# Moved heads third of four pairs in the last image, and layer 3's sums behind the next unit's values

## The chip, the core and the metric

The kernel runs on one core of a Trainium2 chip. A core has a matrix engine (TensorE, PE in the profile; PEld is its weight load), a vector engine (VectorE, DVE), an engine for functions such as exp (ScalarE, ACT), a slower general engine (GpSimd, POOL), and a queue processor that only issues DMAs (SyncE, SP). They share an on-chip memory of 128 partitions (SBUF); matmul results go to a small second memory of eight banks (PSUM). The metric is the device time of one execution in microseconds; a lower number is better.

## The reference, cut to what matters

The input x has 8 images of 384 channels of 32 x 32 points (1024 positions). Four layers are added to it in turn, each after a group normalisation. Two of them hold the change.

Layer 0 is a full attention in each image with 8 heads of 48 channels:

```
q, k, v = dwproj(gn(x))                       # depthwise 3x3, batch norm, gelu, 1x1
attn = softmax(q^T k * 48**-0.5)              # 1024 x 1024 for each head
out  = w_out @ (v attn^T);  x = x + bn(out)   # bn: statistics over all 8 images
```

Layer 3 is a deformable attention with 6 heads of 64 channels, whose keys and values come from 256 sampled points:

```
q = q_w @ gn(x);  offsets = conv5x5 stride 2 of q, norm, gelu, 1x1
k, v = kv_w @ bilinear_sample(gn(x), offsets)
x = x + proj_w @ (softmax(q^T k * 64**-0.5) v) + proj_b
```

Layer 1 (between them) mixes four small experts, layer 2 is a 3x3 depthwise and a 1x1 convolution.

## The kernel before

**Order of work.** The code is written in program order; a list scheduler then orders the instructions of each engine by what is ready in its own model, with earlier code preferred, and adds the waits.[...] ACT is kept as written in layer 0's attention.

**Layer 0's attention.** The loop over `steps` goes image by image (b), pair of heads (pr, 0 to 3), half of the 1024 query positions (h), and two blocks of 128 keys at a time (kc). Per step, `scores` of the next step gives four matmuls per block in row and column quarters (s, L638), ACT takes the exp (p, L645), and `weigh` multiplies by the values into two PSUM banks (pav, L653). A column of ones beside each head's values (number `HQ0` = 24 of each group of 32) gives the softmax sum. At the end of a half, `normalise` (L605) adds the two banks (L610, L611), transposes in blocks of 32 x 32 (L614), takes the reciprocal of the sum's column (L615), multiplies (L616) and transposes back (L621 or L624). The step's `todo` list holds other PE work (projections of the next pair, of the next image, `out_project` of the image before); up to four of them are taken at kc = 2.

**Moved heads.** A head has 48 channels, and two heads of a pair take 2 x 48 of 128 rows. Pair 3 therefore holds no rows of its own in `atts`: its q and k rows are gathered from the spare rows of pairs 0, 1 and 2 by `gather_last` (tile ql, two DMAs on SP after each projection), and its result `al` is put by `place_last` into rows 24 to 31 of each group of 32 in the three blocks of `atts`, with 12 small DMAs. `atts[b]` has three blocks of 128 rows, one for each of pairs 0 to 2. For the last half of the last image the 12 DMAs alternate between SP's and ACT's queue.

**Output projection.** `out_project(b, m, h)` loads xh (a piece of x, two buffers), multiplies `wo0` by `atts` (po, L590), copies po to ot (DVE, or ACT for the last image, L601), takes its statistics (bn_stats, L602), stores ot, and `cross` sums a product of xh and ot (L488, L489). For the last image, h = 0 is taken inside the last half's loop, h = 1 after the loop. Then a check of the reciprocals (okt, L742 to L748) decides, through a branch, whether a slow general form is run; it is not run here. `norms` then makes the batch norm of the whole output, the branch is passed, and layer 1 loads its weights (w1).

**Layers 1 to 3.** From here on the work of two images is interleaved by hand. `layer1(b+1)` is a list of 48 units of three matmuls each (ph, L1274; y, L1295). `layers(b)` is a generator of layers 2 and 3 that yields estimates of idle PE time. For images 0 to 5, each time the yields add up to `UNIT` = 2.6, one unit of layer 1 is put in. Image 6 is treated so only up to a marked point (`yield None`); its rest runs beside image 7's layers, two steps of 7 for one of 6, and image 7's rest runs alone.

**Layer 3's attention** has six units (pr, h) for each image. In unit u, GpSimd adds the two exps (p01, L1620), PE multiplies them by the values (pav, L1605, bank `vbank`, of which there is one), DVE transposes pav (tu, L1623), and PE makes the next unit's scores (s, L1589, two 64-row matmuls that can run side by side). After a yield, two matmuls by ones sum p01 (pss, L1631, in the same `vbank`), and DVE divides: transpose (L1636), reciprocal (L1638), product (L1639), transpose (L1642). p, p01 and other tiles come from one set of five buffers (`flat`), which the next image's o tiles use too. At last comes the output product (pf, L1694). In layer 2, DVE runs a 3x3 filter tap by tap (L1370), in layer 3 a 5x5 filter (off, L1485).

## Time and profile before

| | us |
|---|---|
| median of 3 runs | 3717.47 (3716.41 to 3720.61) |
| the profiled execution | 3716.66 |
| its span | 3714.9 |
| layer 0's attention ends (last pav) | 1799.67 |
| last matmul of layer 0's output | ends by 1817.1 |
| layer 1's first matmul | 1839.81 |
| one image of layers 1 to 3 (2061.84 to 2283.68) | 221.84 |
| image 7 alone, from its first scores | 3653.60 to the end |

Times in the profile count from the span's start. The kernel's whole time also has 1.76 us outside the span. A line of the profile names a code line, an engine, the operation, the tile written and the tiles read, the shape, and a count. A float32 matmul appears as two records, so six records are three matmuls. A shape such as 128*64 is the part of the array that a matmul uses; smaller parts can run side by side. The bracket gives idle time before an instruction and what ended it. Because matmul ends are modelled, a PE that is shown as busy can still be working below its rate.

### The profile page before, as it was taken

To read this page: it belongs to the slowest core of one execution; us is meant where nothing else is said; L and a number is where in the kernel's file an instruction comes from. 1 tells how busy PE (TensorE), PEld (TensorE's weight loads), DVE (VectorE), ACT (ScalarE), POOL (GpSimd) and SP (SyncE) were. 2 spreads that over 40 slices of the span, in tenths; PEclk is the share of its full clock that TensorE was granted. 3 is DMA by queue.
4 is the path that set the end of the run, shared out by engine and by line. 5 is a ranking of instruction groups with operands and counts; after the bars stand their busy time and mean duration, and the time that the engine had idled before them with its cause. 6 is when DMAs were issued, how large, how long until landed. Compare 5 with 4: busy or idle time off the path is not lost.

```text
span 3714.9 us, 39037 instructions
## 1 busy us (share of the span) xinstructions
PE 3598.4 (97%) x15587; PEld 1504.2 (40%) x15587; DVE 1810.6 (49%) x2827; ACT 1273.6 (34%) x1524; POOL 195.9 (5%) x162
## 2 busy tenths in 40 slices
PE   7999999999999999999799999999999999999888
PEld 3444333333333333333244444444344444444433
DVE  6776223232323232323336557564764657557564
ACT  2222354545444453544222321323222232322222
POOL 0000100000000000000000010100101010010111
PEclk9999999999999999999899999999999999999898
DMA  6776311121212021212350010110101001010000
GB/s 205 240 249 231 127 55 36 63 56 43 63 40 78 25 75 28 72 28 72 125 201 23 33 51 20 46 42 33 37 23 56 26 33 43 27 51 20 0 34 18
DMA packets 88178, 253.32 MB, mean 68 GB/s; under 512 B 19114, under 2 KB 19706, under 8 KB 87602
## 3 DMA queue, kind: packets, MB, share of 16 engines
q1 hardware_dynamic: 74904, 211.26, 17.1%
q10 hardware_dynamic: 12504, 37.88, 3.0%
q8 instruction: 127, 2.08, 0.2%
q0 software_dynamic: 576, 1.55, 0.1%
q14 instruction: 67, 0.55, 0.0%
HBM read 133.39 MB, written 75.59 MB: 56 GB/s over the span
## 4 chain that ended last, share of the span: by engine, by line
PE 39%; DVE 10%; ACT 1%; issue 1%; DMA 0%; POOL 0%; DVEq 0%; ACTq 0%; POOLq 0%; SPq 0%
PE y L1295 11%; PE ph L1274 8%; DVE y L1370 6%; PE pq L1415 3%; PE pf L1694 3%; PE pw L1378 3%; PE s L1589 3%; PE pav L1605 2%; DVE hd L1260 1%; PE pss L1631 1%; PE pk L1563 1%; PE pv L1572 1%; DVE off L1485 1%; PE xsb L1549 1%; PE px L1438 1%
## 5 line engine op out<-in xcount | busy, mean ns | idle before, releaser
L645 ACT ACTIVATE p<-s 128x1024 f32<-128x1024 f32 x512 | 496.5, 1021 | 507.0 <-PE s L638 506.7
L1295 PE MATMUL y<-hd,w_sb 128*128 128x512 f32 x1080 | 493.1, 600 | 3.5 <-DVE hd L1260 3.5
L653 PE MATMUL pav<-p,vt 64*64 64x512 f32 x4096 | 487.1, 590 | 0.0
L1274 PE MATMUL ph<-h,w_sb 128*128 128x512 f32 x1104 | 484.1, 594 | 0.4 <-DMA w_sb<-in_w_dram 0.4
L638 PE MATMUL s<-qk,qk 48*64 48x512 f32 x3072 | 370.8, 597 | 3.3 <-ACT p L645 3.3
L391 PE MATMUL pk<-st,cw_sb 126*126 126x512 f32 x720 | 320.3, 606 | 12.7 <-DMA st<-pad 10.9
L1274 PEld LDWEIGHTS ph<-h,w_sb 128*128 128x128 f32 x1104 | 207.5, 190 | 259.5 <-issue 255.3
L1295 PEld LDWEIGHTS y<-hd,w_sb 128*128 128x128 f32 x1080 | 198.0, 191 | 248.4 <-issue 238.2
L653 PEld LDWEIGHTS pav<-p,vt 64*64 64x64 f32 x4096 | 156.6, 133 | 285.1 <-issue 285.1
L610 DVE COPY ta<-pav 128x512 f32<-128x512 f32 x64 | 44.3, 692 | 429.0 <-PE pav L653 426.0
L1284 ACT ACTIVATE hd<-ph,b_sb 128x512 f32<-128x512 f32 x180 | 122.6, 681 | 371.3 <-PE ph L1274 371.2
L1370 DVE SCALAR_TENSOR_TENSOR y<-h,tap,y 128x961 f32<-128x961 f32 (+1 forms) x192 | 234.1, 1244 | 0.6
L391 PEld LDWEIGHTS pk<-st,cw_sb 126*126 126x126 f32 x720 | 139.3, 196 | 185.5 <-issue 179.5
L1485 DVE SCALAR_TENSOR_TENSOR off<-q,dw_sb,off 128x225 f32<-128x225 f32 (+3 forms) x432 | 212.3, 549 | 1.7
L638 PEld LDWEIGHTS s<-qk,qk 48*64 48x64 f32 x3072 | 108.7, 133 | 231.1 <-issue 192.0
L78 DVE COPY qk<-pq 128x512 f32<-128x512 f32 x48 | 33.2, 692 | 292.8 <-PE pq L572 292.8
L397 ACT COPY y<-pk 126x512 f32<-126x512 f32 (+1 forms) x136 | 76.2, 583 | 249.2 <-PE pk L391 111.9
L1596 ACT ACTIVATE p<-s 128x1024 f32<-128x1024 f32 x96 | 93.1, 1021 | 169.5 <-PE s L1589 169.4
L1260 DVE TENSOR_TENSOR hd<-hd,cb 128x512 f32<-128x512 f32 x180 | 122.7, 687 | 48.7 <-ACT hd L1284 48.2
L590 PE MATMUL po<-att,wo_sb 128*128 128x512 f32 x288 | 132.8, 615 | 11.6 <-DMA att<-al 11.6
L1378 PE MATMUL pw<-y,upw 128*128 128x512 f32 x288 | 130.5, 606 | 5.0 <-DVE y L1370 5.0
L572 PE MATMUL pq<-g,wq_sb 128*128 128x512 f32 x288 | 131.5, 607 | 2.0 <-ACT g L494 2.0
(286 smaller groups left out, 3870.2 us busy)
## 6 DMA issues: line engine op xcount, KB each, us to landing
g<-raw SPq DMA_DIRECT2D x72, 512.0 KB
st<-pad SPq DMA_DIRECT2D x180, 168.0 KB
raw<-y ACTq DMA_DIRECT2D x171, 168.0 KB
xa<-in_x_dram SPq DMA_DIRECT2D x24, 512.0 KB
xh<-in_x_dram SPq DMA_DIRECT2D x48, 256.0 KB
f<-in_x_dram SPq DMA_DIRECT2D x24, 512.0 KB
f<-o SPq DMA_DIRECT2D x24, 512.0 KB
o<-ot SPq DMA_DIRECT2D x42, 256.0 KB
```

The lines of the kernel that those rows point to most:

```text
L391: nc.tensor.matmul(pk[h].rearrange("p (h w) -> p h w", w=W)[: 3 * nch, :, o0 : o0 + c1 - c0], lhsT=lhs, rhs=rhs, start=(k == 0), stop=(k = ...
L572: nc.tensor.matmul(pq, lhsT=w_in[v][:, c, pr * P : (pr + 1) * P], rhs=acts[b][v][:, c, h * HALF : (h + 1) * HALF], start=(c == 0), stop=(c ...
L590: nc.tensor.matmul(po, lhsT=wo0[:, c, m * P : (m + 1) * P], rhs=atts[b][:, c, hs], start=(c == 0), stop=(c == KC - 1),)
L638: nc.tensor.matmul(s[64 * k : 64 * k + 64, j * HALF : (j + 1) * HALF], lhsT=kt[r, k0 : k0 + 64], rhs=qt[r, h * HALF : (h + 1) * HALF], sta ...
L645: nc.scalar.activation(p, s, AF.Exp, scale=scale)
L653: nc.tensor.matmul(pav[k][64 * j : 64 * j + 64, :], lhsT=vts[b % 2][r, kc, 2 * hd : 2 * hd + 2, :].rearrange("p a b -> p (a b)"), rhs=p[r, ...
L1260: nc.vector.tensor_tensor(hd, hd, state["cb"], ALU.mult)
L1274: nc.tensor.matmul(ph, lhsT=w1[:, e, c, dc * P : (dc + 1) * P], rhs=state["h1"][c], start=(c == 0), stop=(c == KC - 1),)
L1295: nc.tensor.matmul(y, lhsT=w2[:, e, dc, m * P : (m + 1) * P], rhs=state[h, k], start=(k == 0), stop=(k == NE * KC - 1),)
L1370: nc.vector.scalar_tensor_tensor(d, f, tap2[:, c, t : t + 1], d, ALU.mult, ALU.add)
L1378: nc.tensor.matmul(pw[h], lhsT=upw2[:, c, m * P : (m + 1) * P], rhs=y[c][:, hs], start=(c == 0), stop=(c == KC - 1),)
L1485: nc.vector.scalar_tensor_tensor(d, f, dw3[:, t : t + 1], d, ALU.mult, ALU.add)
```

## The change

In layer 0, last image only, the pairs run in the order 0, 1, 3, 2. The moved heads of pair 3 would then be overwritten by pair 2's result, so those that belong in block 2 go, by the same DMAs, into a free part of the other image's value tile (`spare(0, h)`). In pair 2's first half, two block transposes on DVE turn them into the layout of tu (`spare(1, h)`). Pair 2's `normalise` writes only its own 24 of each 32 columns there, and its last transpose brings both into `atts`. All 12 DMAs are on SP. The two fetches that stood at the third pair stand at the third still, and the first half of the last image's output at the last unit.

In the very last half, `normalise` works in two halves of 256 columns, and the output projection (now into three banks, in two rounds of nine half-width matmuls) follows them. bn_stats reads PSUM instead of ACT's copy there. The check of the reciprocals is put behind the last transpose.

In layer 3, the sums of unit u - 1 come behind the values of unit u, in a bank of `fbank` (three banks, shared with layer 1), and the division of u - 1 behind the transpose of u. tu takes two tiles in turn, in the room of om0 and om1. There is one yield of `UNIT` after the first scores and one in each unit; the number of yields is the same.

```diff
@@ place_last
-            queues[k % len(queues)].dma_start(
-                out=dst[q : q + HS0, k // 4, :], in_=src[r : r + HS0, :]
-            )
+            to = dst[:, k // 4, :] if k < 8 or third is None else third
+            nc.sync.dma_start(out=to[q : q + HS0, :], in_=src[r : r + HS0, :])
@@ out_project(b, m, h, po=None)
-            nc.vector.bn_stats(ost[:, m, 2 * b + h, :], ot)
+            nc.vector.bn_stats(ost[:, m, 2 * b + h, :], ot if po_new else po)
@@ normalise
+        def spare(k, h):
+            vf = vts[B % 2].rearrange("p t h d -> p (t h d)")
+            return vf[:, (2 * k + h) * HALF : (2 * k + h + 1) * HALF]
...
+            tv, tf = tu, tuf
+            if b + 1 == B and pr == 2:
+                tf = spare(1, h)
+                tv = tf.rearrange("p (a b) -> p a b", b=32)[:, :, :HQ0]
+            n = 2 if b + 1 == B and pr == 2 and h == 1 else 1
+            for k in range(n):
+                qs, qb = (slice(k * m // n, (k + 1) * m // n) for m in (HALF, 16))
+                nc.vector.tensor_copy(ta[:, qs], pav[0][:, qs])
+                nc.vector.tensor_tensor(ta[:, qs], pav[1][:, qs], ta[:, qs], ALU.add)
+                nc.vector.transpose(tuf[:, qs], ta[:, qs])
+                nc.vector.reciprocal(rec[:, u, qb], tu[:, qb, HQ0])
+                w = tv.shape[2]
+                nc.vector.tensor_tensor(
+                    tv[:, qb], tu[:, qb, :w],
+                    rec[:, u, qb].unsqueeze(2).to_broadcast([P, 16 // n, w]), ALU.mult,
+                )
+                dst = al if pr == KC else atts[b][:, pr, h * HALF : (h + 1) * HALF]
+                turned = nc.vector.transpose(dst[:, qs], tf[:, qs])
+            if pr == KC:
+                hs = slice(h * HALF, (h + 1) * HALF)
+                place_last(atts[b][:, :, hs], al, spare(0, h) if b + 1 == B else None)
@@ the loop
+        ORDER = ((0, 1, 2, 3), (0, 1, 3, 2))
-            for b in range(B) for pr in range(NPAIR0) for h in range(2)
+            for b in range(B) for pr in ORDER[b + 1 == B] for h in range(2)
...
+            if b + 1 == B and pr == 2 and h == 0 and kc == NS:
+                for k in range(2):
+                    nc.vector.transpose(spare(1, k), spare(0, k))
...
+        pos = [bank(f"po{B - 1}_{m}_1") for m in range(KC)]
+        for k in range(2):
+            qs = slice(k * HALF // 2, (k + 1) * HALF // 2)
+            for m in range(KC):
+                for c in range(KC):
+                    nc.tensor.matmul(
+                        pos[m][:, qs], lhsT=wo0[:, c, m * P : (m + 1) * P],
+                        rhs=atts[B - 1][:, c, HALF:][:, qs], start=(c == 0), stop=(c == KC - 1),
+                    )
         for m in range(KC):
-            out_project(B - 1, m, 1)
+            out_project(B - 1, m, 1, pos[m])
...
-        nc.vector.tensor_scalar(okt, recf, R_LO, None, ALU.is_ge)
+        with tc.issue_after(turned.ins):
+            nc.vector.tensor_scalar(okt, recf, R_LO, None, ALU.is_ge)
@@ layer3
+            def sums(u, p01):
+                pss = fbank(f"pss3_{b}_{u}")
...
+            ps, due3 = scores(*units[0]), None
+            yield UNIT
+            for u, (pr, h) in enumerate(units):
+                p01 = pl.flat([P, N], f"p01_{b}_{u}")
+                nc.gpsimd.tensor_tensor(p01, ps[0], ps[1], ALU.add)
+                pav = weigh(pr, h, ps)
+                if due3:
+                    pss = sums(due3[2], due3[4])
+                tu = pl.one([P, NG * LS], f"om{u % 2}", f"tu_{b}_{u}")[:, :HALF]
+                tu = tu.rearrange("p (a b) -> p a b", b=32)
+                nc.vector.transpose(tu.rearrange("p a b -> p (a b)"), pav)
+                if due3:
+                    divide(pss, *due3[:4])
+                due3 = pr, h, u, tu, p01
+                if u + 1 < NU3:
+                    ps = scores(*units[u + 1])
+                yield UNIT
+                yield 0.0
+            divide(sums(due3[2], due3[4]), *due3[:4])
             yield 3.0
```

`divide` holds the four DVE instructions of before (L1636 to L1642).

## The prediction

> **What bounds the kernel now.** I read the page first, then the waits of TensorE, then the timeline of TensorE where the waits fall, then the stages.

> ```profile
> span 3714.9 us, 39037 instructions
> PE 3598.4 (97%) x15587; PEld 1504.2 (40%) x15587; DVE 1810.6 (49%) x2827; ACT 1273.6 (34%) x1524; POOL 195.9 (5%) x162
> ```

> TensorE (PE) is the bound. Only time in which it idles, runs at a low clock, or runs badly packed can be won. The waits of PE name one place that the change touches in layer 0 (total, times, longest):

> ```profile
> PE po L590 <- DMA att<-al: 11.6, 4, 7.9
> PE pav L1605 <- ACT p L1596: 5.2, 8, 1.5
> ```

> The timeline of PE there, the end of the last image's attention (start, duration, records):

> ```profile
> 1777.34 1.90 PE L653 MATMUL pav<-p,vt 64*64 64x512 f32 x16
> 1780.60 1.10 PE L590 MATMUL po<-att,wo_sb 128*128 128x512 f32 x2 [1.36 <-DMA att<-al]
> 1783.19 1.86 PE L590 MATMUL po<-att,wo_sb 128*128 128x512 f32 x2 [1.49 <-DMA att<-al]
> 1785.96 8.39 PE L590 MATMUL po<-att,wo_sb 128*128 128x512 f32 x14 [0.92 <-DMA att<-al]
> 1794.28 1.95 PE L638 MATMUL s<-ql,ql 48*64 48x512 f32 x16
> ...
> 1807.52 9.57 PE L590 MATMUL po<-att,wo_sb 128*128 128x512 f32 x18 [7.86 <-DMA att<-al]
> ```

> The stage view of the same two stretches (length; busy PE, PEld, DVE, ACT, POOL; clock; DMA share; GB/s):

> ```profile
> 1779.24:1794.28 15.04, 11.27 (x20) 3.97 (x19) 3.85 (x6) 1.17 (x2) 0.00 (x0) 0.77 0.21 62
> 1799.67:1817.10 17.43, 9.58 (x20) 4.25 (x20) 10.98 (x19) 1.17 (x2) 0.00 (x0) 0.80 0.14 33
> ```

> A full-rate 128x512 record takes 0.43 us in this trace (72 records of y in 30.90 us on the chain), so 18 records of po need 7.7 us. The first half of po held PE for 15.04 us, the second ended 17.4 us after the last pav. The clock column (0.77 and 0.80, against 1.00 in the stretches before) shows that the pauses also slow the matmuls behind them.

> Layer 3 shows no such wait; there the loss is in the packing. The last image's attention, PE alone, then VectorE (DVE) beside it:

> ```profile
> 3676.08 1.94 PE L1605 MATMUL pav<-p,vt 128*64 128x512 f32 x8
> 3677.94 1.98 PE L1589 MATMUL s<-q,kt 64*128 64x512 f32 x6
> 3680.02 1.08 PE L1631 MATMUL pss<-p,ones 128*64 128x512 f32 x4
> 3681.03 1.12 PE L1589 MATMUL s<-q,kt 64*128 64x512 f32 x2
> 3682.08 1.94 PE L1605 MATMUL pav<-p,vt 128*64 128x512 f32 x8
> ```

> ```profile
> 3676.18 2.12 DVE L1639 TENSOR_TENSOR tu<-tu,rec 128x512 f32<-128x512 f32 x1
> 3679.16 0.72 DVE L1623 STREAM_TRANSPOSE tu<-pav 128x512 f32<-128x512 f32 x1
> 3681.13 0.72 DVE L1636 STREAM_TRANSPOSE ts<-pss 128x512 f32<-128x512 f32 x1 [1.26 <-PE pss L1631]
> ```

> pav(u+1) and pss(u) share one PSUM bank, so tu, pss, ts, the next pav follow each other: pss starts at 3680.02 after tu (3679.16 + 0.72), pav at 3682.08 after ts (3681.13 + 0.72). While it waits, the scheduler issues one score matmul alone (x2). Two score matmuls in different row halves run side by side (8 records in 1.92 us), a lone one takes 1.05. One unit thus costs 6.0 us with PE marked busy throughout.

> [...] pav (8 records, two column halves side by side, 1.71 us of work) to the next phase takes 1.87, pss 1.01 for 0.85, y (6 records, 2.56) takes 2.77: 0.15 to 0.21 us per change. pav and pss are both 128*64.[...] the product at L1639 takes 2.12 us beside the Pool sum (2.35 us) and 0.68 where none runs.

> **Part 1, layer 0, first half of po.** The order 0, 1, 3, 2 puts the 12 DMAs of the moved heads a unit ahead of po. What po(m,0) waits for is now pair 2's own normalise. Today's normalise of this half runs from 1772.40 to 1776.39 (six instructions of 0.25 to 0.71 us), and PE reaches po at 1779.24: 2.8 us of slack. Added before it in DVE's queue are two transposes of 0.71 us that wait for the third block's DMAs. Those of half 1 follow al, which one unit (13.75 us) earlier is ready at 1762.65; SP takes 8.06 us for the 12 issues and the last po wait today ended 9.5 us after al, so they land near 1772.2; two transposes end by 1773.7 and normalise by 1777.7, still before 1779.24. Gain 15.04 - 7.7 = **7.3 us**. If that cover fails, each us of DMA beyond 1.5 costs one.

> **Part 2, second half.** From the last pav's end (T = 1799.67), normalise in halves: copy and add of 256 columns about 0.5 each, transpose 0.45, reciprocal 0.2, product 0.4, transpose 0.45 (estimates: half of the 512-column rows plus their fixed part) give 2.5; PE starts po at T+2.7 instead of T+7.85. The first nine half-width matmuls take 3.84 us, longer than the second half of normalise, the second nine as much: end T+10.5 (before T+17.25). Half-width records cost nothing extra (18 pk records of 256 columns took 3.87 us, 0.215 each). bn_stats now reads PSUM beside ACT's copy and saves 0.6. What is late next is the third xh tile: it has two buffers, and its load was issued at 1815.08, when the first block's reduce ended. Now that reduce ends near T+10.0, the load lands about 2.3 us later (estimate: at most 3.3, since its user ran at 1818.35), so DVE waits until T+12.4 and reaches the first instruction of the norm (L160) at T+14.3 instead of 1820.12 = T+20.45. Gain **6.1 us** (5 to 7.4). The check of the reciprocals (0.68 + 1.18 + 1.22 us) moves behind the last transpose, beside po. What follows (norm, branch, w1's load of 9.0 us) shifts as a whole.

> **Part 3, what the new order takes forward.** Pair 3's scores need the last gathered rows of q. Those are issued on SP at 1724.96 and 1725.5, behind one 512 KB fetch (1724.13), and pair 3's first scores now stand where s of pair 2 ran, 1727.51. The gather lands 2 to 4 us after issue (estimate from the burst that ends by 1731), the pav behind the score in PE's queue waits with it: cost **1.5 us** (0 to 4). The two fetches keep their third place.

> **Part 4, layer 3, images 0 to 5.** From the first s (2151.22) to pf (2197.08) lie 45.86 us with 30 y records. Work: s 10.24, pav 10.24, pss 5.12, y 12.8 = 38.4; the rest is 27 mode changes, two lone scores (1.7 us) and an ACT wait (0.55). After the change a unit is pav + pss in one mode (2.56 + 0.16), s 1.92, y 2.77 = 7.41, with 36 y records (the last unit came after pf before). Sum: 1.92 + 2.77 + 6.56 + 4 x 7.41 + 2.72 + 0.85 = 44.5, against 45.86 + 2.56 = 48.4. That is 3.9; if pav to pss costs a change, 3.0. I take 3.6 each: 6 x 3.6 = **21.6 us** (9 to 24). Everything is PE time: in one period (2061.84 to 2283.68) PE is busy 220.89 of 221.84 us. The exps lie under y, the Pool sum under y and pav. No instruction is added; the DVE chain of the previous unit has 7 us where it needs 4.6.

> **Part 5, image 7 alone.** No y fills here. pav + pss 2.72 and s 1.92 give 4.64 us a unit; DVE needs 0.72 x 2 + 0.25 + 2.12 + 0.71 = 4.5, so 4.75 is fair. pav(0) to pav(5) took 30.7 us (3657.19 to 3687.92); now 5.2 + 4 x 4.75 = 24.2. Gain **6.5 us** (3 to 7). The end, with 36 pf records, stays.

> **Part 6, image 6 beside 7.** PE saves some changes, but each division comes one unit later, where DVE is the bound (off taps, 3575 to 3622), and one more Pool sum may stretch a tap (one took 1.92 instead of 0.4). Net 0 (-4 to +4).

> Sum: 7.3 + 6.1 - 1.5 + 21.6 + 6.5 = 40.0 us. The profiled execution took 3716.66 (1.76 outside its span): 3676.7. The median is 0.8 above it: **3677**.

> **Rivals.**
> Forecast, 0.55: 3667 to 3690.
> Layer 3 gains half: the scheduler again splits scores or y while it waits for tu or the sums. For it: a list scheduler produced such splits at 2166.36 and 2179.95. Against: the shared bank that caused them is gone. 40 - 14 - 3 = 23 us, 3695; 0.17.
> The DMAs eat layer 0: gather 4 us, transposes late, xh late; 12 us less, 3689; for it the 2.8 us of slack only. 0.07.
> More: layer 2 starts earlier because the last y precedes pf, and changes cost less; 52 us, 3665; 0.06.
> Nothing beyond the bound of 0.2% (7.4 us, what a measurement of this kernel can tell): 0.05.
> Slower, 0.10: VectorE's queue blocked by the o loads. p01 lives one unit longer and the five flat buffers are held longer, so the next image's three o tiles (issued from 2183.04, used by DVE at 2189.60, 2192.43 and 2194.97, already 0.3 and 0.6 late) are loaded later; if their L1220 stands in DVE's queue ahead of the last divisions, pf waits. It decides from 40/6 = 6.7 us per image; at 9 us, 3677 + 54 = 3731. Against: the loads need to be only before the ph at 2215.

> The range 3664 to 3704 leaves out the slower case, some of no change and a little below. Faster 0.85, same 0.05, slower 0.10.

> **What would show it.** po with no DMA wait and 7.7 us for its first half at clock 1.00; pav followed by pss, s whole (x8), then y x6, with periods of 7.4 us; 4.7 us a unit in the last image; the step from pf to pf 3.6 us below 222.0. Wrong: lone s records, DVE waits for o in the attention, a DVE wait ahead of pair 2's normalise.

## The result, and the profile after

The changed kernel takes 3687.61 us (median of 4, 3684.65 to 3690.41), the kernel before beside it 3717.67 us (median of 4). The ratio is 0.9919, with a 95% interval of 0.9904 to 0.9933: 30 us faster. The forecast was 3677 us in a range of 3664 to 3704; the sign and the range held, the gain was put a third too high. The profiled execution took 3684.65 us, the shortest of the four, with a span of 3682.8 us, 32.1 below that of before.

The page after, its span and the row of the bounding engine (busy us, share, instructions):

```profile
span 3682.8 us, 39040 instructions
PE 3569.8 (97%) x15605; PEld 1525.8 (41%) x15605; DVE 1765.5 (48%) x2835; ACT 1273.8 (35%) x1524; POOL 196.1 (5%) x162
```

Busy PE fell by 28.6 us: most of the gain is not idle time but matmul time. Some 4.6 us of it is po at a higher clock (its last two stretches kept PE busy 11.27 and 9.57 us before, with a clock of 0.77 and 0.80 over the stretch, and 7.92 and 8.31 after, with 1.00 and 0.97), the rest in the main better packing, as the prediction had it. The waits of TensorE after (engine, line waited for: total us, times, longest):

```profile
PE pw L1410 <- DVE y L1402: 9.3, 8, 3.0
PE pom L1543 <- ACT off L1522: 7.7, 1, 7.7
PE pf L1737 <- DVE att L1664: 3.8, 1, 3.8
PE pav L1637 <- ACT p L1628: 3.4, 7, 1.5
```

The 11.6 us of po on the moved heads are gone. New is pf on DVE (3.8, once, in image 6). The wait of pw on layer 2's taps has grown from 5.0 to 9.3, that of pom (layer 3's offsets) from 6.7 to 7.7.

The timeline of TensorE at the end of layer 0, and the stage view of the two stretches that were 15.04 and 17.43 us (the second now begins at the last pav's end and reaches the first instruction of the norm, 20.45 us before):

```profile
1729.60 2.06 PE L654 MATMUL s<-ql,ql 48*64 48x512 f32 x16 [1.60 <-DMA ql<-qk]
...
1781.42 7.99 PE L591 MATMUL po<-att,wo_sb 128*128 128x512 f32 x18
1789.34 1.95 PE L654 MATMUL s<-qk,qk 48*64 48x512 f32 x16
1791.11 3.62 PE L669 MATMUL pav<-p,vt 64*64 64x512 f32 x32
1794.65 2.86 PE L764 MATMUL po<-att,wo_sb 128*128 128x256 f32 x12
1798.01 5.45 PE L764 MATMUL po<-att,wo_sb 128*128 128x256 f32 x24 [0.50 <-DVE att L640]
```

```profile
1781.42:1789.34 7.92, 7.92 (x21) 3.33 (x19) 3.85 (x6) 1.17 (x2) 0.00 (x0) 1.00 0.24 68
1794.65:1808.10 13.45, 8.42 (x42) 7.05 (x38) 13.12 (x30) 1.76 (x3) 0.00 (x0) 0.97 0.26 79
```

The first half of po has no wait and the full clock. The second half begins at once: its first twelve records (six matmuls, of blocks 0 and 1) don't need pair 2. Its end is set by DVE (13.12 of 13.45 us busy). The price of the new order is the 1.60 us ahead of the first ql score.

A unit of an early image in layer 3, TensorE:

```profile
2162.23 1.99 PE L1621 MATMUL s<-q,kt 64*128 64x512 f32 x8
2164.15 2.84 PE L1327 MATMUL y<-hd,w_sb 128*128 128x512 f32 x6
2166.92 1.94 PE L1637 MATMUL pav<-p,vt 128*64 128x512 f32 x8
2168.69 1.03 PE L1650 MATMUL pss<-p,ones 128*64 128x512 f32 x4
2169.65 1.99 PE L1621 MATMUL s<-q,kt 64*128 64x512 f32 x8
```

A unit is 7.42 us, scores are whole, and pav to pss (both 128*64) is 1.77 us from start to start, where pav to the scores (64*128) was 1.87 before: next to no change of mode, which here and below means the array shape that a record names.

To split the gain, the executions are laid side by side at a matmul that lies ahead of every edit: a query projection of the last image in layer 0 (12 records with wq, at 1650.71 before, 1651.01 after). Below, "layer 0" runs from there to the first ph of layer 1; "period" is the mean step of the first scores of images 0 to 5; "image 6" runs from the query projection of image 6 in layer 3 (the seventh pq; the texts on record below call it image 7's) to the first scores of image 7; "image 7" from there to the end of the span; "all" is from the common matmul to the end. One execution each, us:

| kernel | layer 0 | period | image 6 | image 7 | all |
|---|---|---|---|---|---|
| before | 189.10 | 221.99 | 260.09 | 61.30 | 2064.2 |
| after | 178.17 | 218.93 | 260.82 | 57.17 | 2031.8 |

From before to after: layer 0 -10.9, five periods -15.3, the sixth -3.0, image 6 +0.7, image 7 -4.1, and +0.2 in what lies between; together -32.4. The common matmul comes 0.3 us later after, so the spans differ by 32.1.

The stage times repeat well where no chance comes in: with the changed layer 3 the period is 218.88 to 218.94 in five profiles. Layer 0 and image 6 vary more: the changed layer 0 takes 176.90 to 178.17 us in eight profiles (mean 177.5), that of before 188.97 to 189.39 in three. So layer 0 gained 11.6 us in the mean, and the 10.9 of the pair above is at the low end.

### The profile page after: what moved, and what is told of

Same layout as the page of the kernel before. It is cut to its first block, busy times and chain, and to the rows that moved or that the text cites. A ratio compares the mean times of both kernels' runs of the same rounds, so it can differ in the third digit from the quotient of the medians.

```text
span 3682.8 us, 39040 instructions
## 1 busy us (share of the span) xinstructions
PE 3569.8 (97%) x15605; PEld 1525.8 (41%) x15605; DVE 1765.5 (48%) x2835; ACT 1273.8 (35%) x1524; POOL 196.1 (5%) x162
## 4 chain that ended last, share of the span: by engine, by line
PE 40%; DVE 9%; ACT 1%; DMA 0%; issue 0%; POOL 0%; DVEq 0%; POOLq 0%; ACTq 0%; SPq 0%
PE y L1327 12%; PE ph L1306 8%; DVE y L1402 6%; PE pq L1447 3%; PE pf L1737 3%; PE pw L1410 3%; PE pav L1637 2%; PE s L1621 2%; DVE hd L1292 1%; PE pss L1650 1%; PE pk L1595 1%; PE pv L1604 1%; PE xsb L1581 1%; PE px L1470 1%; DVE off L1517 1%; PE plog L1056 0%
## 5 line engine op out<-in xcount | busy, mean ns | idle before, releaser
L391 PE MATMUL pk<-st,cw_sb 126*126 126x512 f32 x720 | 320.5, 607 | 11.2 <-DMA st<-pad 10.4
L669 PEld LDWEIGHTS pav<-p,vt 64*64 64x64 f32 x4096 | 165.4, 133 | 276.3 <-issue 268.1
L630 DVE COPY ta<-pav 128x512 f32<-128x512 f32 (+1 forms) x65 | 44.2, 682 | 411.1 <-PE pav L669 411.1
L1737 PE MATMUL pf<-att,wp_sb 128*128 128x512 f32 x288 | 130.3, 607 | 4.3 <-DVE att L1664 3.8
```

The lines of the kernel that those rows point to most:

```text
L391: nc.tensor.matmul(pk[h].rearrange("p (h w) -> p h w", w=W)[: 3 * nch, :, o0 : o0 + c1 - c0], lhsT=lhs, rhs=rhs, start=(k == 0), stop=(k = ...
L669: nc.tensor.matmul(pav[k][64 * j : 64 * j + 64, :], lhsT=vts[b % 2][r, kc, 2 * hd : 2 * hd + 2, :].rearrange("p a b -> p (a b)"), rhs=p[r, ...
L1737: nc.tensor.matmul(pf[:, hs], lhsT=wp3[:, pr, m * P : (m + 1) * P], rhs=att[:, pr, hs], start=(pr == 0), stop=(pr == NPAIR3 - 1),)
```

## The experiments

The first two experiments and the last three were timed four or five times each; the seven between were run once, and are read by their stages.

**The two halves alone.** The layer 0 of the changed kernel with the layer 3 of before, and the reverse. The edit of the first, against the changed kernel (the second is its mirror image on the kernel before):

```diff
-            ps, due3 = scores(*units[0]), None
-            yield UNIT
+            ps = scores(*units[0])
...
-                if due3:
-                    pss = sums(due3[2], due3[4])
...
+                pss = vbank(f"pss3_{b}_{u}")
```

> Layer 0 of the changed kernel with layer 3 of the kernel before. Theory A (the two halves of the change add up, and the traces' own split is right): layer 0 is shorter by 10.6 us, with po's first half in 7.9 us instead of 15.0 (-7.1), the end of the second half 7.0 us earlier, ql's gather at +1.6, and about +1.4 in w1's load; total about 10.6 us below the kernel before, ratio 0.9971. Theory B (the recorded sum 7.3 + 6.1 - 1.5 holds for layer 0, and w1's load is only noise of one execution): 11.9 to 12.0 below, ratio 0.9968, w1's load back near 9.0 us. Theory C (layer 0 carries little, the gain is all in layer 3): within 4 us of the kernel before.

> Layer 3 of the changed kernel with layer 0 of the kernel before. Theory A (halves add up): about 21.5 us below the kernel before (ratio 0.9942): 3.1 us in each of the six image periods (218.9 instead of 222.0), about -1 in image 6, about +4 in image 7 alone, about -1 at its end. Theory B (the recorded 21.6 + 6.5 = 28.1 holds for layer 3 and layer 0 disturbs it): 28 below, periods of 218.4, 4.75 us a unit in image 7. Its w1 load, with layer 0 as before, tells whether 10.4 us belongs to the new layer 0 (then 9.0 here) or to chance (then either).

Measured: layer 0 alone 0.9961 (0.9946 to 0.9975), layer 3 alone 0.9935 (0.9918 to 0.9951). From the common matmul:

| kernel | layer 0 | period | image 6 | image 7 | all |
|---|---|---|---|---|---|
| layer 0 alone | 177.07 | 222.00 | 257.12 | 61.27 | 2050.5 |
| layer 3 alone | 189.39 | 218.88 | 260.23 | 57.25 | 2042.3 |

Theory A holds in that the two halves add up: layer 3 keeps its period and image 7 without the new layer 0, and layer 0 its time without the new layer 3. Layer 0 alone gained 12.0 us, which is the size of theory B, not of A; w1's part did not go back to 9.0 for it (9.98). The intervals of the two ratios are as wide as what was asked (5 us on either side): in the profiles the common matmul comes anywhere from 1648 to 1660, most of which arises ahead of the first query projection at 391 to 404. What causes it was not tested; the stage times settle the question. One thing came unasked: image 6 takes 257.12 here and 260.09 in the profile of before, with the same layer 3. The last section shows why; against the undisturbed 257.1 the change loses 3 to 4 us in image 6, against the 260.1 of before 0.7.

**The bank alone.** The kernel before, with one line changed:

```diff
-                pss = vbank(f"pss3_{b}_{u}")
+                pss = fbank(f"pss3_{b}_{u}")
```

> The kernel before with one edit: the sums of layer 3 go to another pool of PSUM banks than the next unit's values, with the order of work, the yields and everything else left. Theory A (packing and mode changes are the gain; the shared bank gave only the lone scores): the lone score matmuls go (1.7 us an image), the sums still stand apart from the values, so the period falls from 222.0 to 220.5 or so, and image 7 alone falls by up to 2 us of its 30.7 (5.7 us a unit). Theory B (the shared bank alone was the loss): the period falls to about 219 and image 7 to 5.1 us a unit, as in the whole change. Theory C (the bank was not the loss): nothing moves, 222.0 and 6.0.

Measured: period 219.08, image 6 263.02, image 7 56.61, "all" 2045.5. For the period and image 7 this is theory B: of the 3.06 us that the change gains in a period, the bank alone gains 2.91, with the sums left behind the scores in the source. TensorE in its layer 3:

```profile
2173.28 1.99 PE L1589 MATMUL s<-q,kt 64*128 64x512 f32 x8
2175.20 1.08 PE L1631 MATMUL pss<-p,ones 128*64 128x512 f32 x4
2176.11 1.89 PE L1605 MATMUL pav<-p,vt 128*64 128x512 f32 x8
2177.93 1.99 PE L1589 MATMUL s<-q,kt 64*128 64x512 f32 x8
2179.85 1.08 PE L1631 MATMUL pss<-p,ones 128*64 128x512 f32 x4
```

With a bank of its own, pss(u) stands straight ahead of pav(u+1), in the same mode (0.91 from start to start, where pss to another shape was 1.01 before), and the lone scores are gone: the scheduler reaches the packing from the other side. Attention takes 42.96 us with the fill of before, against 45.88. Where it does worse is image 6.

**The order alone.** The changed kernel with its sums back in the bank of the values:

```diff
-                pss = fbank(f"pss3_{b}_{u}")
+                pss = vbank(f"pss3_{b}_{u}")
```

> The changed kernel, with the sums of layer 3 put back into the pool of banks that the values use; order, yields and joined numbers as changed. Theory A (order and bank are both needed): the sums can no longer follow the values of the next unit at once, they wait for its transpose; lone scores come back, one or two mode changes a unit are added, the period rises from 218.9 to about 220.5 and image 7 from 5.04 to about 6 us a unit. Theory B (bank alone): back to 222.0 and 6.0. Theory C (order alone): 218.9 and about 5.1.

Measured: period 224.19, image 7 61.66, 3721.41 us in its one time. The period is worse than all three theories had it, and worse than before by 2.2 us: the new order (with its fill) without the bank is a loss.

```profile
2170.39 1.94 PE L1637 MATMUL pav<-p,vt 128*64 128x512 f32 x8
2172.26 1.12 PE L1621 MATMUL s<-q,kt 64*128 64x512 f32 x2
2173.31 1.08 PE L1650 MATMUL pss<-p,ones 128*64 128x512 f32 x4
2174.32 1.98 PE L1621 MATMUL s<-q,kt 64*128 64x512 f32 x6
...
2172.38 0.72 DVE L1680 STREAM_TRANSPOSE tu<-pav 128x512 f32<-128x512 f32 x1 [4.08 <-PE pav L1637]
```

The sums (2173.31) must wait until DVE has taken the next values out of the bank (2172.38 + 0.72); one score matmul fills that time alone, now in every unit that has scores to make. A unit is 8.62 us.

**The place of the sums, with the bank.** The changed kernel with the sums and the division issued behind the next scores instead of ahead of them:

```diff
-                if due3:
-                    pss = sums(due3[2], due3[4])
...
                 if u + 1 < NU3:
                     ps = scores(*units[u + 1])
+                if due3:
+                    divide(sums(due3[2], due3[4]), *due3[:4])
```

> The changed kernel, its sums of layer 3 in their own bank as changed, but issued behind the next unit's scores instead of straight behind its values. TensorE's order comes out as in the run with one bank: values, one score matmul, sums, three scores, fill. Theory A (neighbours of one tiling mode are what counts): a unit takes 8.6 us as in that run, against 7.41, the image period comes near 224, and image 7 rises from 5.04 to about 6 us a unit although no bank is shared. Theory B (the shared bank made that run slow by its waits, not the order): the period stays within 1 us of 218.9 and image 7 near 5.1. In between (two mode changes of 0.17 a unit and no lone score): about 220.6.

Measured: period 220.02, image 6 257.78, image 7 58.00. The order that the expectation names did not come out; with its own bank the scores stay whole:

```profile
2183.04 1.94 PE L1637 MATMUL pav<-p,vt 128*64 128x512 f32 x8
2184.91 1.99 PE L1621 MATMUL s<-q,kt 64*128 64x512 f32 x8
2186.83 1.08 PE L1650 MATMUL pss<-p,ones 128*64 128x512 f32 x4
2187.84 2.84 PE L1327 MATMUL y<-hd,w_sb 128*128 128x512 f32 x6
```

A unit is 7.57 us (2183.04 to 2190.61) against 7.42: one change of mode more, so a change is put at 0.15 by this pair. Measured from the changed kernel, the later place costs 0.15 us a unit and 1.1 a period, the shared bank 1.20 a unit (8.62) and 5.3 a period. So theory B is nearer: the bank's wait is the larger part, the neighbours of one mode the smaller.

**The fill.** The changed kernel with the yields of before (2.0, then 0.5 and 1.0 a unit):

```diff
-            yield UNIT
+            yield 2.0
...
-                yield UNIT
-                yield 0.0
+                yield 0.5
+                yield 1.0
```

> The changed kernel with the fill given out as before: 2.0 at the first unit and 0.5 and 1.0 a unit, in place of one whole fill group behind each unit. Theory A (the fill's place hardly matters once values and sums stand together): the fill comes in lumps of six y between units as before, attention and period move by less than 0.7 us, 218.9 stays. Theory B (the even fill is a part of the gain: it hides the exps and the division): waits of values on the exps and of sums on the division appear, 0.5 to 1 us a unit without fill, period 221 or more. Images 6 and 7, which have no fill, stay within 1 us in both.

Measured: period 218.67, image 6 259.60, image 7 56.83. Theory A for the period: how the fill is given out is worth nothing here, 0.26 us the other way. But the attention itself moved by 2.0 us (42.48), as it holds 30 y records again: the sixth group stays outside it, and the wait of pw is back at 5.0 us in all, while pav's on the exps is 7.2 instead of 3.4. Against the bank alone, which has the same yields, the new order gains 0.41 us a period (219.08 and 218.67).

**Image 6.** The changed kernel with the old order in the last two images, image 6 with the shared bank, image 7 with a bank for the sums:

```diff
+            before = b + 2 >= B
...
-                pss = fbank(f"pss3_{b}_{u}")
+                pss = (vbank if b + 2 == B else fbank)(f"pss3_{b}_{u}")
```

> The changed kernel with the units of the last two images in the order of before: image 6 with the shared bank, so as in the kernel before, image 7 with a bank of its own for the sums. Theory A (in image 6 the later divisions leave TensorE idle for 3.8 us ahead of the projection, and the half clock behind that costs as much again): from image 7's pq to image 7's first scores 257 us instead of 260.8, no half-clock stretch behind that projection's start; image 7 from its first scores to the end 56.6 instead of 57.2; together about 4 us less. Theory B (image 6 is set by VectorE's taps whatever the order): within 1 us of 260.8, together about 0.6 less.

Measured: image 6 258.00, image 7 55.92; "all" 2027.7, 4.1 below the changed kernel. This is how image 6 looks in the changed kernel, in the timeline and in the stage view (length; busy PE, PEld, DVE, ACT, POOL; clock; DMA share; GB/s):

```profile
3562.51 3.70 PE L1737 MATMUL pf<-att,wp_sb 128*128 128x512 f32 x8
3569.97 9.85 PE L1737 MATMUL pf<-att,wp_sb 128*128 128x512 f32 x16 [3.76 <-DVE att L1664]
```

```profile
3566.21:3569.97 3.76, 0.00 (x1) 0.00 (x1) 3.76 (x10) 0.00 (x0) 0.00 (x0) 0.82 0.00 0
3569.97:3579.82 9.85, 9.85 (x16) 4.01 (x16) 7.29 (x11) 0.00 (x0) 0.00 (x0) 0.72 0.00 0
```

The timeline shows pf's first 24 records. DVE is busy throughout the wait: the last divisions, each a unit later than before, stand in its queue among the taps of image 7. Then the granted clock falls (0.72 in that stretch), and 16 records take 9.85 us instead of 6.9 (at 0.43). In the experiment the longest wait of pf on DVE's att is 0.5 us. The mechanism of theory A is shown, but 1 us less of it than expected; in that execution another short wait (px, below) was followed by half clock (0.57 over 4 us), which the changed kernel doesn't have.

**Layer 2's head.** One more fill group goes to layer 2 ahead of its projection:

```diff
-        yield 2.0
+        yield 4.6
         for m in range(KC):
             whole, pw = pair(last, f"pw{b}_{m}")
```

> The changed kernel with one more fill group of layer 1 given to layer 2 ahead of its first projection (pw), so that the last unit of the attention has none behind it. Theory A (layer 2 lacks cover since the attention takes 36 y instead of 30): the wait of pw on the taps y, 1.04 us an image, goes, attention loses one group of 2.77 which layer 2 gains, period 218.2 instead of 218.9, about 4 us in all. Theory B (taps on VectorE set layer 2's start anyway, or the last unit's division then lies bare): pw still waits, or pf waits for the division by up to 2.8 us, period 219 to 221.5.

Measured: period 218.49, and attention 42.83 us instead of 44.50. The waits of TensorE in this kernel:

```profile
PE pav L1637 <- ACT p L1628: 5.0, 13, 1.5
PE pss L1650 <- POOL p L1673: 3.4, 7, 0.5
PE pw L1410 <- DVE y L1402: 3.0, 1, 3.0
```

The wait of pw is gone in all images but the last, but the last unit's pav (0.27 us) and pss (0.49), which have no fill now, wait instead. Of pw's 1.04 us, 0.44 a period are left: between the theories. The group itself is only moved: from the first ph to the first scores of image 0 this kernel takes 3.2 us more, and image 6 gets 2.7 back (258.15).

**The gather.** In the last image the next pair's projections go ahead of the output projections:

```diff
-                    todo += [
+                    first = [
                         lambda v=v, q=q, b=b, pr=pr: project(b, pr + 1, v, q)
                         for v in (1, 0) for q in range(2)
                     ]
+                    todo = first + todo if b + 1 == B else todo + first
```

> The changed kernel with one edit in layer 0: in the last image the projections of the next pair are put ahead of the output projections, so that the gather of the last q rows starts about 14 us earlier. Theory A (pair 3's first scores wait for that gather and nothing else): the wait of s on ql, 1.60 us, goes; from the last query projection anchored at the same place, layer 1's first ph comes 1.6 us earlier. Theory B (the gather also waits behind fetches on SP, or the out projections moved back then delay something): the wait stays, or a like one appears elsewhere, 0 us.

Measured: the wait of s on ql is gone:

```profile
1724.80 1.90 PE L654 MATMUL s<-ql,ql 48*64 48x512 f32 x16
```

From the common matmul to the first half of po it takes 128.44 us (130.41 and 129.54 in the two profiles of the changed kernel), layer 0 175.82. Theory A.

**The changed kernel again, and two versions with three edits.** The first version joins the last three diffs, the second takes the yields of before in place of layer 2's fill.

> The changed kernel once more, unedited, on the chip of the two versions below. Theory A (the first timing stands): ratio to before 0.9919, within 0.9904 to 0.9933. Theory B (the two halves timed alone, 0.9961 and 0.9935, add up to more than the whole): 0.990 or less. By the traces from the last image's first query projection to the end, 2031.8 us of 2064.2, theory A.

> The changed kernel with three edits together: the last image's projections first, image 6 as in the kernel before and image 7 in the old order with a bank of its own, and one more fill group ahead of layer 2's projection. Theory A (they add up): 1.6 + 4.1 + 2.6 = 8.3 us below the changed kernel of the same call, 0.9897 of before. Theory B (each only moves waits to its neighbours): within 3 us of the changed kernel.

> As the version above, but with the fill given out as in the kernel before, in place of one more fill group for layer 2. Theory A: 1.6 + 4.1 + 1.5 = 7.2 us below the changed kernel of the same call, 0.9900 of before, period 218.7. Theory B: within 3 us of the changed kernel.

| kernel | median us (range) | ratio to before (95%) | layer 0 | period | image 6 | image 7 |
|---|---|---|---|---|---|---|
| changed, again | 3688.09 (3687.67 to 3691.53) | 0.9918 (0.9904 to 0.9931) | 176.90 | 218.88 | 261.40 | 57.15 |
| with fill | 3678.50 (3678.08 to 3678.71) | 0.9890 (0.9875 to 0.9905) | 174.77 | 218.49 | 255.34 | 56.09 |
| with old yields | 3680.66 (3672.34 to 3684.79) | 0.9888 (0.9873 to 0.9903) | 176.09 | 218.60 | 261.25 | 57.78 |

The changed kernel repeats. Both versions are below it by 9.6 and 7.4 us in the median, where 8.3 and 7.2 were expected: theory A. The interval of the first ratio overlaps that of the changed kernel by 0.0001, that of the second not at all. Both beat both kernels; the first is the steadier. The profile of the second was its slowest execution: it held half clock behind px in image 6 (6.8 us of it) and again up to the first scores of image 7.

## Why the prediction was right, and where it was wrong

- **Part 1, the first half of po: right.** 15.04 became 7.92: 7.1 us where 7.3 stood, at clock 1.00, with no wait on a DMA. The spare transposes show no wait on TensorE.
- **Part 2, the second half: right in sum.** The stretch to the norm lost 7.0 us, against 6.1. The start was missed: the prediction held all of po back until T+2.7, but blocks 0 and 1 of att are ready, and 12 of the 36 records ran during the normalise. The term "w1's load of 9.0 us shifts as a whole" was wrong by about 1: from its issue to the first ph pass 9.1 to 9.4 us in the three profiles with the old layer 0, and 8.9 to 11.2 (mean 10.3) in the eleven with the new one. In five of these ph waits 0.1 us or less: TensorE works on plog, the product of layer 1's gate, until then, whose 52 records take 7.8 to 8.9 us there against 7.6 in the old ones, since the clock stays at half longer (up to 5.4 us from plog's start, 2.9 before). In the other six ph waits 0.9 to 1.4 us for w1; why it lands later is not settled. What each edit in the very last half brings was not measured alone.
- **Part 3, the gather: right.** 1.60 us and, in the repeat, 0.74, against 1.5; it goes when the gather starts earlier. Parts 1 to 3 together: 11.9 us forecast, 10.9 in the profiled pair, 11.6 in the mean of the profiles.
- **Part 4, images 0 to 5: the attention right, the period 0.5 short.** The attention was worked out as 44.5 us and takes 44.50, and pav to pss costs next to no change of mode (1.77 against 1.87 to the scores). The failing term is what the six y records were taken from. They lay at layer 2, where they covered the taps: pw waited 0.30 us on them before and 1.04 after. Of 3.9 us, 3.06 are left, where 3.6 was taken: 18.3 us in six images, against 21.6. With one fill group given back to layer 2 the period is 218.49, 3.5 below before. The reading of the cause, one bank for sums and values, is shown twice (bank alone -2.9, order alone +2.2). But the prediction credited bank and joined order together with the gain, and the bank alone brings nearly all of it: at the same yields the order adds 0.41.
- **Part 5, image 7 alone: mechanism right, a wait left out.** From first to last pav 30.73 became 25.59, -5.1 against 6.5. The prediction summed TensorE's work to 4.64 us a unit, put DVE beside it at 4.5, with its product at 2.12 beside the Pool sum (0.69 in the last unit, where none runs), and took 4.75. It gave no time to the exp between scores and values. From the trace of a unit after, all engines:

```profile
3642.47 1.99 PE L1621 MATMUL s<-q,kt 64*128 64x512 f32 x8
...
3643.64 1.95 ACT L1628 ACTIVATE p<-s 128x1024 f32<-128x1024 f32 x2 [3.10 <-PE s L1621]
...
3644.16 0.69 DVE L1661 TENSOR_TENSOR tu<-tu,rec 128x512 f32<-128x512 f32 x1
3644.72 1.08 PE L1637 MATMUL pav<-p,vt 128*64 128x512 f32 x4 [0.27 <-ACT p L1628]
...
3645.67 2.35 POOL L1673 TENSOR_TENSOR p<-p,p 128x1024 f32<-128x1024 f32 x1 [2.69 <-ACT p L1628]
```

  The Pool sum starts behind the second exp, when the product (0.69) is over; DVE needs 3.04 us of a unit. What sets it is scores, exp, values: 2.25 us from s to pav, where 1.92 was taken, then 2.79 for pav and pss, 5.04 in all, with 0.27 of it idle. In the old order with its own bank (the version with fill) pss stands between s and pav and covers the exp, and a unit takes 4.6 to 4.9 us. "The end stays" failed too, by 1.0 us from the start of the last pav to the end: before, four of the 36 records of pf ran in the gaps ahead of the last sums, two of them ahead of the last pav; after, all 36 stand behind the last sums, which wait 0.49 us on Pool. Image 7 in all: -4.1.
- **Part 6, image 6: in its range, at its bad end.** 0 was taken, from -4 to +4. The profiles show 0.7 us lost, or 3 to 4 against an execution of the old layer 3 without the half clock at px. The prediction named the divisions in DVE's queue, and set them off against the saved changes of mode; what it left out is TensorE's clock behind the 3.76 us that pf waits for them (0.72 over the next 9.85 us). The change also takes the 2.84 us of px away, and adds 1.77 us for tu ahead of the last pav and 1.0 to pom's wait. How these add up was not measured; with the old layer 3 and the same wait of px, two executions differ by 3.0 us in image 6 (260.09 and 257.12), with half clock behind px in the longer one alone.
- **The rivals.** Neither scores nor y split again in the changed kernel, the fetches of o delayed nothing, so the two rivals of half the gain and of a blocked queue fell (pf has no wait in images 0 to 5). The missing 7.9 us of the profile are 3.3 in part 4, 2.4 in part 5, 0.7 in part 6, 0.5 in part 2 with w1's load, 0.3 in parts 1 and 3, and 0.7 in stretches that no part named: small errors, nearly all on one side, as Part 2 gained more than was forecast before w1. The medians differ by 2 us less than the profiles, since the profiled execution was the shortest of its kernel.

## What to carry to other kernels

Before reordering work around a shared PSUM bank, give one of the two tiles another bank and look at the order that results: one line brought 2.9 of 3.1 us a period here (and did worse in image 6), and the reordering alone lost 2.2. When fill is moved into a stage, price the stage that it is taken from: here the taps of layer 2 lay bare by 0.7 us an image. A division moved one unit later left pf without a wait in images 0 to 5; in image 6 it stood behind taps, and TensorE paid for the wait twice, by the idle time (3.76 us) and by the clock after it (0.72 over 9.85 us).

## What the runs showed of the hardware

The same wait cost nothing in one execution and 3 us in another. In image 6 of the kernel before, px (in layer 3, a multiplication of h by the identity) waits 2.84 us for DVE's copy; with the changed layer 0 and the same layer 3 the wait is 2.84 as well. First before, then layer 0 alone, with stage views (length; busy PE, PEld, DVE, ACT, POOL; clock; DMA share; GB/s) whose stretches follow the grid that is told of below:

```profile
3584.05 0.55 PE L1438 MATMUL px<-ident_sb,h 128*128 128x128 f32 x3 [2.84 <-DVE xT L78]
...
3578.86:3582.28 3.42, 2.35 (x13) 1.16 (x11) 3.42 (x6) 1.98 (x3) 1.88 (x1) 1.00 0.00 0
3582.28:3585.69 3.41, 1.64 (x6) 0.66 (x7) 2.97 (x7) 0.68 (x1) 0.50 (x1) 1.00 0.00 0
3585.69:3589.10 3.41, 3.41 (x10) 1.57 (x11) 3.40 (x8) 0.68 (x1) 0.00 (x0) 0.50 0.00 0
```

```profile
3580.29 0.55 PE L1470 MATMUL px<-ident_sb,h 128*128 128x128 f32 x3 [2.84 <-DVE xT L78]
...
3575.34:3578.75 3.41, 2.10 (x11) 1.05 (x11) 3.41 (x5) 1.73 (x3) 2.11 (x1) 1.00 0.00 0
3578.75:3582.17 3.42, 1.88 (x9) 0.91 (x10) 2.99 (x7) 0.68 (x1) 0.26 (x1) 1.00 0.00 0
3582.17:3585.58 3.41, 3.41 (x17) 1.10 (x15) 3.29 (x8) 0.67 (x1) 0.00 (x0) 1.00 0.00 0
```

In one the clock falls to 0.50 for 6.8 us, from 1.6 us behind the wait on; in the other it stays at 1.00. From the first scores of image 6 to those of image 7 it takes 127.67 and 124.47 us.

The stretch that half clock followed before was not idle throughout: PE was busy for 1.64 of its 3.41 us. A change of mode cost 0.15 us here (7.57 against 7.42 us a unit). The kernel that issues one score matmul of each unit alone took 1.05 us a unit more than the one that keeps the scores whole (8.62 against 7.57), with one change of mode more.
